# Two graph-attention layers on one core: new issue tables, no negated weights, other first loads and last operations

## The chip, the cores and the metric

The kernel runs on one core of one Trainium2 chip. The metric is the device time of one execution in microseconds (us), the smaller the better. All data are float32.

A core has five engines that run beside each other and wait for each other only through semaphores. TensorE (PE in the profile; its weight loads are PEld) multiplies matrices. VectorE (DVE), ScalarE (ACT) and GpSimd (POOL) do the elementwise work. SyncE (SP) issues DMA transfers; ACT and POOL can issue them too.

## The reference

There are 128 graphs of 128 nodes with 512 features each: `x` is (128, 128, 512) and `adj` is (128, 128, 128). Each layer is attention with 8 heads of 64 over the nodes of a graph, weighted by the adjacency:

```
layer 0:  q, k, v = x W_q + b_q, x W_k + b_k, x W_v + b_v
          e   = exp(q k' / 8 + c) * (adj + eps)      c, gate: from x and w_g
          x1  = x + gate * (e v) / rowsum(e)
layer 1:  q, k, v = x1 Wq + bq, x1 Wk + bk, x1 Wv + bv
          e   = exp(q k' / 8) * max(adj, 1e-8)
          o   = (e v) / rowsum(e)
          out = layernorm(x1 + o Wo + bo; gamma, beta)
```

That is seven projections of 16,384 rows by a 512 x 512 matrix, and 2 x 128 x 8 small attentions. A test on the row sums (`good`, `bad`) runs along and at the end decides on a branch that these inputs don't take.

## The kernel before, in words

**Tiles and stages.** Four graphs make a group (G = 4), 32 groups a layer (NG = 32). Group t runs from 0 to 63: 0 to 31 are layer 0, 32 to 63 layer 1. Per group the kernel loads x turned (features on partitions, tile `xT`) and natural (`xn`), forms sums of its blocks on POOL, makes v, q and k, scores, softmax weights and the mixed values. In layer 0 the result x1 goes to memory twice, natural (`x1d_n`) and in blocks of 32 x 32 (`x1d_b`). In layer 1 the mixed values go to memory in blocks and come back turned:

- `store_blocks` writes `x1d_o` in four stores of 128 KB (packets of 128 bytes) for each half of the group;
- `load_mixed` reads each half back into `GW` (512 KB, tile `gw`), and DVE transposes its 32 x 32 blocks;
- POOL forms sums (`innerB`, `innerT`), and `o_matrix` multiplies by Wo;
- `residual` adds x1 with an accumulating DMA of 512 KB on POOL's own queue (`h<-x1d_n`), two per group; `norm_and_store` normalises and stores.

All other transfers of the steady groups are issued by SP, in order, on one queue (q1).

**Strassen on two levels.** A projection is seven products of half-size blocks (class `Strassen`). P6 and P7 are multiplied plainly, P1 to P5 by seven quarter-size products each (`inner`). The weight side needs sums of weight blocks: `combine_outer` (on DVE for layer 0's v, q and k, on POOL for layer 1) and `combine_inner` (POOL). The x side needs `outer_sums` and `inner_sums` on POOL. In the kernel before, the weight block A22 was kept negated (`NA22`), by a `tensor_scalar_mul` in `combine`.

**Order.** The function records every operation in an object `Plan`, which finds what must precede what. `tabled` gives each operation a due time out of a table and issues them by due time, as soon as their predecessors are out; `issue` (L523) does it, so nearly all lines of the trace are L526. This fixes each engine's program order; the hardware then only waits for semaphores. There are five tables of due times in hundredths of a microsecond: FIRST (groups 0 to 2), the pattern for groups 3 to 29 (one table with a start and a period), CHANGE (groups 30 to 35), the pattern for groups 36 to 60, and LAST (61 to 63 and the closing part). 20,907 operations are placed so.

**Places that the change touches.** The beginning of `fast_path`: the first loads of x (`load_natural(0)`), of W_v, W_q and W_k (`weights`), of w_g into `GW`, and of the row b_v (`ROW`), whose sum with the first v products runs on DVE. The change of layers: at group 32 `weigh_rows(c)`, for c from 0 to 3, builds b_v Wo from quarters of Wo in `GW[:, 2]`. The closing part: group 62's four graphs still need their layer norm (`HU`) while group 63 (`HL`) is worked graph by graph. `begin_one` and `finish_one` do the norm of one graph with two DVE instructions; `ordinary` does it with a scaling on ACT (`scale`) and two POOL instructions (`rows`), after a `shift` on POOL. The last instructions are the norm of graph 3 of group 63, its store, and the test `bad`.

Of the kernel before, what the change touches and what calls it, by code (L numbers as in the profile page):

```python
# [42 lines left out]
class Strassen:  # L43


    A11, A12, S4, NA22, S1, S2, S3 = range(7)
    OPERANDS = {
        "P1": (A11, "B11"), "P2": (A12, "B21"), "P3": (S4, "B22"), "P4": (NA22, "T4"),
        "P5": (S1, "T1"), "P6": (S2, "T2"), "P7": (S3, "T3"),
    }  # L50
    SUMS = {"T1": ("B12", "B11"), "T2": ("B22", "T1"), "T3": ("B22", "B12"), "T4": ("T2", "B21")}
    RAW = {(0, 0): A11, (1, 0): A12, (1, 1): NA22, (0, 1): S3}
    INSIDE = ("P1", "P2", "P3", "P4", "P5")

    @staticmethod
    def load(engines, t, w):

        q = w.rearrange("(k c p) (m e) -> k m p c e", k=2, p=P, m=2)
        for n, ((k, m), i) in enumerate(Strassen.RAW.items()):
            engines[n % len(engines)].dma_start(t[:, i], q[k, m])  # L60

    @staticmethod
    def combine(v, a11, a12, a21, na22, s1, s2, s4, part=None):


        if part != 1:
            v.tensor_tensor(s1, a21, na22, ALU.add)
            v.tensor_tensor(s2, s1, a11, ALU.subtract)
        if part == 0:
            return  # L70
        v.tensor_tensor(a21, a11, a21, ALU.subtract)
        v.tensor_tensor(s4, a12, s2, ALU.subtract)
        v.tensor_scalar_mul(na22, na22, -1.0)

    @staticmethod
    def combine_outer(v, t, part=None):
        w = Strassen
        w.combine(v, *(t[:, i] for i in (w.A11, w.A12, w.S3, w.NA22, w.S1, w.S2, w.S4)), part)
# [10 lines left out]
    def inner_weight(t, x, i):  # L89
# [13 lines left out]
    (3, 29, 71.95, 41.905, [int(v) for v in '''  # L103
        0 2091 1819 2159 3282 230 115 1491 1245 2355 2023 2457 1887 2274 3842 1559 2389 1423 1955 3593 6418 4033
        4374 5817 9269 9422 5963 6533 3925 4295 5277 4424 3674 4548 5140 5208 5071 5401 5916 5847 5470 5682 5516
        5984 6537 7217 6661 7498 7301 8277 7582 7836 8361 8644 7933 9588 9748 10550 9913 10045 10788 5025 5081 5149
        5176 5213 5281 5344 5412 5475 5522 5650 5694 5738 5803 5888 5105 5257 5354 5381 5432 5500 5585 5653 5781
        5828 6059 6190 6234 6529 6680 5917 6146 6215 6241 6299 6385 6442 6525 6573 6619 6652 6738 6806 6833 6870
        6938 7001 7070 7111 7157 7228 6753 6914 7173 7200 7367 7452 7498 7763 7859 7906 6595 6783 6801 6820 7740
        6343 6886 6916 6960 7425 8271 8679 7872 8789 7982 7133 7653 8094 7369 7534 8582 8821 8840 8859 8947 7717  # L110
        8431 8518 8734 9071 9202 9312 9469 9694 9579 13385 11897 13425 6422 6485 6554 6580 6693 6761 6826 6895 7045
        7091 7137 7410 7454 7585 7629 7754 7800 6706 6782 6850 6877 6958 7026 7067 7289 7345 7391 7881 7947 7991
        8078 8340 8386 7470 7541 7610 7636 7673 7742 7816 7884 7925 7971 8025 8122 8190 8217 8254 8322 8385 8453
        8494 8541 8673 8432 8516 8600 8627 8680 8800 8987 9055 9097 9143 7978 8034 8103 8129 8209 8277 8341 8409
        8472 8519 8564 8724 8768 8855 8899 8967 9013 8058 8165 8234 8261 8297 8366 8429 8497 8560 8612 9118 9184
        9228 9315 9383 9471 8726 8811 8880 8907 8943 9012 9053 9121 9162 9209 9262 9359 9427 9454 9491 9624 9688
        9773 9819 9865 9936 9517 9578 9651 9678 9731 10140 10293 10361 10468 10514 10037 10449 10596 10274 10387
    '''.split()]),
    (36, 60, 1503.84, 52.968, [int(v) for v in '''
        0 1486 1548 492 2912 3531 445 3872 4580 5040 4709 3569 3679 4902 5164 5274 5526 5347 5868 4374 5233 5416  # L120
        5595 4153 4276 4295 4055 4184 4214 4587 4697 4367 4477 4405 4827 5030 4641 4771 5174 5297 5450 4988 5176
        5306 5632 5946 5522 5836 8015 11828 13160 4196 4361 4429 4456 4660 4729 5087 5155 5404 5450 5535 5645 5798
        5885 5953 4526 4704 4783 4810 4945 5185 5360 5428 5513 5560 6104 6169 6278 6322 6390 5632 5688 5756 5783
        5841 5910 5972 6041 6147 6194 5922 6016 6084 6111 6235 6303 6366 6434 6497 6543 6614 6450 6519 6587 6614
        6694 6762 6825 6906 6956 7003 5698 5754 5822 5849 5929 5997 6060 6128 6213 6294 6340 6453 6563 6650 6781
        6850 6895 6266 6410 6478 6505 6606 6675 6869 6937 7022 7068 6978 7087 7240 7284 7352 7398 6687 6738 6806
        6833 6912 6981 7044 7129 7175 7221 7309 7371 7472 7498 7546 7640 7699 7768 7852 7899 7981 7444 7503 7571
        7598 7656 7724 7809 7960 8094 8148 7075 7131 7199 7226 7328 7405 7459 7527 7590 7636 7682 7765 7874 7962
        8005 8086 8132 7141 7197 7265 7292 7415 7557 7612 7680 7743 7789 8203 8247 8400 8487 8555 8601 7862 7918
        7986 8013 8050 8118 8159 8270 8378 8424 8058 8116 8184 8215 8291 8359 8444 8512 8575 8649 8731 8647 8695  # L130
        8776 8803 9024 9092 9155 9280 9330 9420 8812 9177 9301 9048 9161 5079 5931 6324 6327 7282 7343 7569 7698
        6407 7890 7426 7500 8384 8140 8208 10130 10268 10754 7822 8577 9836 8935 8232 8334 8402 8429 8531 8599 8640
        8710 8782 8889 9067 9111 9199 9549 9653 8504 8597 8675 8702 8739 8807 9242 9490 9636 9750 10045 10088 10154
        10198 10266 9149 9286 9354 9521 9592 9713 9914 10047 10132 10187 10513 10570 10638 10665 10723 10807 10898
        10983 11029 11075 11146 10339 10427 10496 10540 10613 10682 10766 10835 10876 10922 11004 12447 13042 12723
        12845 13327 13341 13362 13574 13743 13915 14342 13595 13750 14039 14473 11862 13338 13436 12875 13400 13464
        13497 13588 13667 14015 14590 14719 14117 14843 15008 15401
# [3 lines left out]
        1538 7625 29872 1229 1777 0 0 47 47 141 141 188 94 94 914 470 517 0 410 484 510 584 460 534 560 645 423 235  # L141
        799 752 4549 705 611 1620 658 564 3469 1233 329 4220 4293 376 26047 21079 24140 7653 14131 706 886 1006 1619
        1870 1126 1438 2293 2051 2826 2706 3007 3420 3788 3668 851 980 727 1414 1104 1479 1249 1381 1653 2858 1885
        2280 3298 4667 2800 3277 5251 5481 4451 4604 5553 610 653 697 741 826 1178 1222 1265 1309 1377 872 916 1003
        1091 1558 1484 1528 1572 1615 1739 1047 1353 1397 1440 1810 1921 1965 2009 2052 2171 2271 2315 2490 2577
        2645 545 2106 2677 2152 2050 2009 2276 2759 2322 3075 2194 4245 4163 5113 2363 2420 2466 3132 2512 3242 1797
        2553 1844 4907 5760 785 828 959 1134 1443 1541 1746 1790 2096 2140 2244 2342 1659 1703 1834 1878 1990 2533
        2621 2665 2708 2776 2822 2358 2402 2446 2839 2946 3058 3102 3145 3233 3360 3189 3277 3495 3539 3607 1373
        2924 4369 5719 5195 4286 4948 5375 6230 4616 2635 5416 4328 6065 3422 5636 6783 6866 7031 7363 2235 2594
        4673 3034 5926 2883 2927 2971 3014 3082 3128 3364 3408 3451 3583 3651 3714 2184 2227 2752 2796 3176 3845  # L150
        3889 3932 3976 4044 4090 3626 3714 3801 4064 4138 4238 4282 4370 4413 4504 4195 4844 4931 4975 5136 3861
        5885 4989 6024 6520 1566 1612 5983 2718 7265 5030 6617 7584 7321 7893 4204 4575 6825 7419 6727 4122 5154
        5678 5595 8459 4632 4969 5217 4868 5017 961 1348 1029 846 2232 1484 1416 1165 1667 2413 1850 1097 2054 1918
        3237 1552 1735 1986 1280 3298 7196 8688 3218 7308 8755 9468 3516 282 3479 3608 4783 3737 2965 3173 4012 3902
        4714 5526 5458 5816 3971 4081 5071 4410 6271 6663 6395 6557 8266 8445 7460 7630 8922 9243 8142 8383 9386
        9518 8640 8774 9590 3687 3758 3826 3853 4020 4088 4151 4281 4326 4372 4457 4501 4544 4888 4956 3249 3320
        3389 3415 3670 3908 4107 4199 4348 4443 5106 5150 5194 5237 5336 4516 4588 4729 4756 5019 5196 5325 5397
        5511 5588 4576 5063 5131 5158 5675 5808 5850 5918 5959 6005 6087 5409 5467 5568 5594 5719 5787 5893 6066
        6193 6271 5369 5580 5664 5829 6106 5533 5656 5674 5693 7072 8619 7203 9353 7543 7309 5981 6456 6715 6327
# [369 lines left out]
def fast_path(ctx, tc, args, GOOD, bad):  # L529
# [3 lines left out]
    nc = Plan(tc)  # L533
# [816 lines left out]
```

## Time and profile before

| | |
|---|---|
| median of 3 runs | 3109.75 us (3105.86 to 3109.96) |
| profiled execution, own time | 3109.7 us |
| its span | 3107.9 us, granted clock 0.998 |
| PE busy | 3061.0 us, 98% |
| DVE, POOL, ACT busy | 2290.9, 2240.3, 1803.5 us |
| DMA | 341.87 MB, q1 42.1% and q0 (POOL's) 6.3% of 16 engines' span |
| longest groups | layer 0: a period of 41.9 us; layer 1: of 53.0 us |

The span is the time from the first to the last instruction of the profiled execution; 1.8 us of the own time lie around it. Busy times say how long an engine was at work, not whether it was waited for. As nearly all instructions stand on one line, the profile is read by tiles and by windows of time here, one window for each group or stage.

### The profile page before, as it was taken

How to read it: one execution, taken by the hardware profiler on the slowest of the kernel's cores; microseconds unless marked ns; L12 is line 12 of the kernel's file. 1: busy time of each engine (PE TensorE's matmuls, PEld its weight loads, DVE VectorE, ACT ScalarE, POOL GpSimd, SP SyncE). 2: the span in 40 equal slices, each digit the busy share in tenths (PEclk: the TensorE clock that was granted, in tenths of full speed). 3: DMA queues.
4: the chain of work that ended last, by engine and by line, in shares of the span. 5: the costliest groups of instructions: out<-in, count | busy, mean ns of one | idle time of the engine just before them, and what ended most of it. 6: DMA issues, size and time to landing. Idle time of an engine off the chain costs nothing.

```text
span 3107.9 us, 121261 instructions
## 1 busy us (share of the span) xinstructions
PE 3061.0 (98%) x50394; PEld 2665.0 (86%) x50394; DVE 2290.9 (74%) x5075; ACT 1803.5 (58%) x5179; POOL 2240.3 (72%) x2713
## 2 busy tenths in 40 slices
PE   8999999999999999999999999999999999999997
PEld 6888888888888888878888888888888888888885
DVE  5777777777777777766777777777777777777776
ACT  3666666666666666644555556565655555555653
POOL 8777666667666666689686867777786868687775
PEclk9999999999999999999999999999999999999999
DMA  4655555555555555444435353535444453535343
GB/s 117 129 118 112 112 116 117 113 124 113 111 108 118 114 120 117 100 134 103 105 95 123 86 131 81 124 87 123 94 113 105 102 115 93 124 83 130 81 106 101
DMA packets 963098, 341.87 MB, mean 110 GB/s; under 512 B 864240, under 2 KB 871408, under 8 KB 962544
## 3 DMA queue, kind: packets, MB, share of 16 engines
q1 hardware_dynamic: 944272, 299.48, 42.1%
q0 software_dynamic: 16864, 32.51, 6.3%
q8 instruction: 396, 6.49, 0.9%
q10 hardware_dynamic: 1408, 2.10, 0.2%
q14 instruction: 158, 1.29, 0.1%
HBM read 192.42 MB, written 141.56 MB: 107 GB/s over the span
## 4 chain that ended last, share of the span: by engine, by line
PE 74%; POOL 11%; DMA 8%; SPq 2%; issue 2%; DVE 2%; ACT 1%; ACTq 0%; POOLq 0%; DVEq 0%
PE bankA L526 36%; PE s L526 13%; PE bankB L526 13%; PE bankC L526 13%; DMA x1d_o<-o 4%; POOL h L526 3%; DMA gw<-x1d_o 3%; POOL T L526 2%; SPq L526 2%; POOL innerB L526 1%; POOL xn L526 1%; POOL innerT L526 1%; DVE gw L526 1%; ACT h L526 0%; POOL xT L526 0%
## 5 line engine op out<-in xcount | busy, mean ns | idle before, releaser
L526 PE MATMUL bankA<-T,w 128*64 128x256 f32 (+1 forms) x4232 | 541.0, 351 | 1.1 <-ACT bankA L526 1.1
L526 DVE TENSOR_TENSOR bankA<-bankA,s 128x128 f32<-128x128 f32 x868 | 255.5, 295 | 325.8 <-PE bankA L526 199.4
L526 PEld LDWEIGHTS bankA<-T,w 128*64 128x64 f32 x4232 | 273.2, 137 | 37.5 <-ACT bankA L526 1.6
L526 ACT ACTIVATE bankA<-ident 128x256 f32<-128x256 f32 x434 | 168.1, 387 | 197.4 <-DVE v L526 61.9
L526 POOL TENSOR_TENSOR gw<-xn,gw 128x512 f32<-128x512 f32 x128 | 162.9, 1279 | 162.0 <-ACT gw L526 93.5
L526 POOL TENSOR_TENSOR gw<-w,gw 128x512 f32<-128x512 f32 x128 | 163.5, 1283 | 155.3 <-ACT gw L526 110.2
L526 PE MATMUL bankA<-w,T 128*64 128x256 f32 (+1 forms) x2116 | 273.4, 351 | 0.0
L526 DVE TENSOR_TENSOR bankB<-bankB,s 128x128 f32<-128x128 f32 x650 | 191.2, 294 | 104.2 <-PE bankB L526 92.1
L526 PE MATMUL s<-qT,kT 64*128 64x128 f32 x4096 | 263.1, 278 | 0.0
L526 PEld LDWEIGHTS s<-qT,kT 64*128 64x128 f32 x4096 | 238.6, 188 | 28.3 <-issue 22.3
L526 DVE TENSOR_TENSOR bankC<-bankC,s 128x128 f32<-128x128 f32 x652 | 191.2, 293 | 96.4 <-PE bankC L526 48.8
L526 PE MATMUL bankC<-xT,w 128*64 128x128 f32 (+1 forms) x2296 | 229.2, 279 | 0.1
L526 ACT COPY s<-bankA 128x128 f32<-128x128 f32 x434 | 114.6, 264 | 192.4 <-PE bankA L526 135.8
L526 ACT ACTIVATE gw<-gw 128x512 f32<-128x512 f32 x256 | 161.6, 632 | 109.1 <-POOL gw L526 109.1
L526 ACT ACTIVATE bankC<-ident 128x256 f32<-128x256 f32 x326 | 125.0, 383 | 163.3 <-DVE v L526 50.2
L526 POOL TENSOR_TENSOR xn<-gw 128x512 f32<-128x512 f32 x62 | 79.3, 1279 | 137.2 <-PE bankA L526 131.9
L526 DVE STREAM_TRANSPOSE xT<-xT 128x512 f32<-128x512 f32 x252 | 173.3, 696 | 2.4 <-issue 2.4
L526 ACT ACTIVATE s<-s,c 128x1024 f32<-128x1024 f32 x128 | 139.7, 1092 | 55.2 <-PE s L526 55.2
L526 PE MATMUL bankA<-w,xn 128*64 128x256 f32 x1364 | 168.3, 350 | 0.0
L526 ACT COPY s<-bankB 128x128 f32<-128x128 f32 x325 | 86.4, 266 | 139.6 <-PE bankB L526 137.8
L526 PEld LDWEIGHTS bankC<-xT,w 128*64 128x64 f32 x2296 | 142.1, 137 | 25.3 <-ACT bankC L526 16.0
L526 POOL TENSOR_TENSOR innerB<-gw 128x256 f32<-128x256 f32 x31 | 22.5, 727 | 194.7 <-DVE gw L526 194.7
(268 smaller groups left out, 10183.8 us busy)
## 6 DMA issues: line engine op xcount, KB each, us to landing
xT<-x1d_b SPq DMA_DIRECT2D x64, 512.0 KB, 4.8
xT<-in_x_dram SPq DMA_DIRECT2D x496, 64.0 KB, 3.6
x1d_o<-o SPq DMA_DIRECT2D x248, 128.0 KB, 3.9
gw<-x1d_o SPq DMA_DIRECT2D x62, 512.0 KB, 4.3
h<-x1d_n POOLq DMA_DIRECT2D x62, 512.0 KB, 8.0
out_dram<-h SPq DMA_DIRECT2D x60, 512.0 KB, 3.9
xn<-in_x_dram SPq DMA_DIRECT2D x32, 512.0 KB, 4.7
x1d_b<-w SPq DMA_DIRECT2D x128, 128.0 KB, 3.5
```

The lines of the kernel that those rows point to most:

```text
L526: self.tc.keep_in_program_order(getattr(getattr(self.nc, engine), method)(*args, **kw))
```

## The change

It has five parts.

1. **No negated weights.** A22 is kept as loaded; the sum T4 is B21 − T2 in place of T2 − B21. The `tensor_scalar_mul` of `combine` is gone: 39 on POOL (35 of 128x128, 4 of 128x512) and 3 on DVE (128x512).
2. **First loads.** x and W_v are loaded by turns, two halves of x and two quarters of W_v at a time, on SP and ACT; the row b_v follows at once, ahead of W_q.
3. **`weigh_rows(0)`** runs on ACT in place of DVE (two instructions of 128x256).
4. **Last operations.** Graphs 3 and 0 of group 62 take `ordinary` after one more `shift`, in place of `begin_one` and `finish_one`: four DVE instructions become two on ACT and four on POOL (five with the shift), and the store of graph 3 goes from ACT's to SP's issue.
5. **New tables.** All five tables of due times are others. The matmuls are the same in number and shape, 25,181 calls; 20,868 operations are placed in all. The periods stay at 41.905 and 52.97. In layer 1's pattern, counted from the group's first `xT` load, the transfers and what follows them are due at:

| due after the first xT load, us | before | after |
|---|---|---|
| two `residual` loads, POOL's queue | 4.1, 12.7 | 1.05, 3.11 |
| last four `x1d_o` stores | 2.25, 3.35, 5.39, 6.49 | 2.39, 3.03, 3.67, 4.31 |
| second reload `gw<-x1d_o` | 10.30 | 8.75 |
| DVE's transposes of it | 19.85, 20.46 | 16.79, 17.40 |
| POOL's first sum from it | 21.29 | 18.23 |

The second xT load and the adjacency are due at 4.96 and 5.41 after the change.

```diff
     def combine(v, a11, a12, a21, a22, s1, s2, s4):
+        v.tensor_tensor(s1, a21, a22, ALU.add)
+        v.tensor_tensor(s2, s1, a11, ALU.subtract)
         v.tensor_tensor(a21, a11, a21, ALU.subtract)
         v.tensor_tensor(s4, a12, s2, ALU.subtract)
-        v.tensor_scalar_mul(na22, na22, -1.0)
...
-    SUMS = {"T1": ("B12", "B11"), "T2": ("B22", "T1"), "T3": ("B22", "B12"), "T4": ("T2", "B21")}
+    SUMS = {"T1": ("B12", "B11"), "T2": ("B22", "T1"), "T3": ("B22", "B12"), "T4": ("B21", "T2")}
...
-    (3, 29, 71.95, 41.905, [int(v) for v in '''
+    (3, 29, 75.15, 41.905, [int(v) for v in '''
...
-    (36, 60, 1503.84, 52.968, [int(v) for v in '''
+    (36, 60, 1510.52, 52.967, [int(v) for v in '''
...
-CHANGE = 18.03, [int(v) for v in '''
+CHANGE = 16.42, [int(v) for v in '''
...
-LAST = 2828.05, [int(v) for v in '''
+LAST = 2830.01, [int(v) for v in '''
...
-            nc.gpsimd.tensor_tensor(t4, t2, b21, ALU.subtract)
+            nc.gpsimd.tensor_tensor(t4, b21, t2, ALU.subtract)
...
             if c == 0:
-                nc.vector.tensor_scalar(o, w, b, None, ALU.mult)
+                nc.scalar.activation(o, w, AF.Identity, scale=b)
...
-    load_natural(0, nc.sync, nc.scalar)
-    weights(WV, 0, 0, w_v0, nc.sync, nc.scalar)
+    for k in range(2):
+        load_natural(0, nc.sync, nc.scalar, pairs=(k,))
+        weights(WV, 0, 0, w_v0, nc.sync, nc.scalar, quarters=slice(2 * k, 2 * k + 2))
+    nc.sync.dma_start(ROW, b_v0.partition_broadcast(P))
     weights(WQ, 0, 1, w_q0)
...
     load_adjacency(0)
-    nc.sync.dma_start(ROW, b_v0.partition_broadcast(P))
...
-    begin_one(u, 3, HU[3])
-    finish_one(u, 3, HU[3])
+    shift(u, slice(0, 2))
+    ordinary(3)
...
-    begin_one(u, 0, HU[0])
-    finish_one(u, 0, HU[0])
+    ordinary(0)
```

## The prediction

> **What bounds the kernel now.** I read first the page's busy times and its chain of work, then the windows query over single groups, then the waits, the timeline and the chain of waits wherever a window showed TensorE short of full.
>
> ```profile
> PE 3061.0 (98%) x50394; PEld 2665.0 (86%) x50394; DVE 2290.9 (74%) x5075; ACT 1803.5 (58%) x5179; POOL 2240.3 (72%) x2713
> PE 74%; POOL 11%; DMA 8%; SPq 2%; issue 2%; DVE 2%; ACT 1%; ACTq 0%; POOLq 0%; DVEq 0%
> ```
>
> TensorE is busy for 3061.0 of 3107.9 us. The change leaves every matmul in place, so it can win only TensorE's idle time: 46.9 us, of which about 15 lie behind the last real matmul. The chain says who holds it up: POOL and DMA, hardly DVE. Where it idles is read from windows of one group each (columns: window, length, then busy us of PE, PEld, DVE, ACT, POOL, granted clock, DMA share, GB/s):
>
> ```profile
> 0.00:71.95 71.95, 63.40 (x736) 47.74 (x738) 40.91 (x69) 21.95 (x58) 59.80 (x99) 1.00 0.54 127
> 71.95:113.86 41.91, 41.91 (x708) 36.97 (x704) 28.93 (x67) 27.34 (x77) 36.64 (x47) 1.00 0.60 126
> 1371.00:1413.00 42.00, 36.48 (x436) 26.62 (x434) 25.81 (x40) 9.12 (x21) 35.84 (x54) 0.96 0.09 14
> 1821.60:1874.60 53.00, 51.35 (x855) 45.11 (x850) 38.77 (x88) 29.04 (x82) 38.06 (x47) 1.00 0.47 107
> 2139.50:2192.40 52.90, 52.90 (x885) 46.87 (x883) 40.60 (x92) 30.92 (x88) 39.76 (x50) 1.00 0.46 107
> 3039.90:3092.90 53.00, 49.63 (x602) 35.15 (x600) 37.13 (x78) 21.54 (x59) 36.24 (x44) 1.00 0.32 82
> 3092.90:3107.90 15.00, 0.19 (x2) 0.09 (x2) 8.36 (x16) 0.98 (x5) 3.80 (x5) 0.64 0.39 143
> ```
>
> Layer 0's steady group is full (41.91 of 41.91), so a new pattern there can win nothing. In layer 1 some groups are full (2139.50) and some are not (1821.60). The rest of the loss is in the start, the change of layers and the end.
>
> The start, from TensorE's timeline (in brackets: idle before, and what ended it):
>
> ```profile
> 8.77 1.95 PE L526 MATMUL bankA<-w,xT 128*64 128x256 f32 x16 [1.65 <-DMA w<-in_L_gnn_W_v_dram]
> 16.03 1.95 PE L526 MATMUL bankA<-w,wi 128*64 128x256 f32 x16 [1.44 <-DVE w L526]
> 20.61 0.65 PE L526 MATMUL bankA<-w,wi 128*64 128x256 f32 x4 [1.34 <-DVE u L526]
> 50.53 0.44 PE L526 MATMUL bankC<-w,xT 128*64 128x128 f32 x4 [2.97 <-POOL xT L526]
> ```
>
> That is 7.4 us in four stalls. Behind the second and third is DVE's `t<-bankA,row`, which sat 3.57 us until the row b_v landed at 14.50; the row is only the 13th load on SP.
>
> The change of layers, all engines:
>
> ```profile
> 1370.05 0.46 POOL L526 TENSOR_TENSOR wi<-w,wi 128x128 f32<-128x128 f32 x1
> 1370.06 6.30 DVE L526 TENSOR_SCALAR gw<-w,bv 128x256 f32<-128x256 f32 x1
> 1372.51 3.71 POOL L526 TENSOR_TENSOR w<-w 128x512 f32<-128x512 f32 x3
> 1376.28 0.68 DVE L526 TENSOR_TENSOR v<-bankB,u 128x512 f32<-128x512 f32 x1
> 1377.06 0.69 PE L526 MATMUL bankB<-w,xT 128*64 128x256 f32 x2 [5.52 <-issue]
> ```
>
> `weigh_rows(0)`'s product takes 6.30 us while POOL runs sums without a break; its twin at 1381.78 takes 0.31. Behind it in DVE's order is the v sum that frees bank B, and TensorE idles 5.52 us.
>
> Layer 1, from the chain of waits:
>
> ```profile
> 1851.07 8.91 DMA x1d_o<-o
> 1860.04 7.11 DMA gw<-x1d_o
> 1867.81 0.67 DVE gw L526
> ```
>
> The mixed output goes to memory in blocks and comes back: store 8.91, reload 7.11 (the page's medians are 3.9 and 4.3), and then DVE's transpose starts late. Counted from the first xT load of each group, the second reload lands at 20 to 22 us in most groups and DVE is ready for it at about 20.3: no margin. The TensorE gaps that follow are 0.1 to 1.6 us and sum to about 7.5 over groups 36 to 60.
>
> The tail:
>
> ```profile
> 3091.86 1.75 DVE L526 SCALAR_TENSOR_TENSOR xT<-xT,rs,beta 128x512 f32<-128x512 f32 x1 [0.87 <-POOL rs L526]
> 3101.04 0.34 ACTq L526 DMA_DIRECT2D out_dram<-h  x1
> 3101.41 0.14 DVE L526 TENSOR_SCALAR bad<-bankC 1x1 int32<-1x1 f32 x1 [0.28 <-PE bankC L526]
> ```
>
> After the last real matmul (3092.6) DVE's normalisations run to 3101, then `bad`, and 6.35 us after `bad` the span ends; the last store lands at 3103.10, before that.
>
> **What the Trainium skill says.** "VectorE: DVE Perf Modes", section "Mode 2×_2P — use both read ports for one tensor": a product of one SBUF tensor with a scalar takes both of VectorE's read ports. "GPSIMD Engine Reference", section "1. Specifications": GpSimd shares its SBUF interfaces with VectorE, and contends with such an instruction or with one of two SBUF inputs. The trace agrees: 6.30 against 0.31 us. "DMA: Bandwidth & Descriptors", section "Queues, rings and completion order": each DMA engine takes turns between queues packet by packet. The trace fits: stores of 128-byte packets on q1, 3.9 us by median, take about 9 whenever `residual`'s 512 KB load on POOL's queue runs beside them.
>
> **The change part by part** (us against the profiled execution: span 3107.9, own time 3109.7, which is also the median of the three runs, 3109.75).
>
> *No negated weights.* POOL loses 35 products of 0.53 and 4 of 1.49, 24.5 us; DVE loses 3 of 0.66 to 0.96. T4 = B21 − T2 costs what T2 − B21 did. In the steady groups there are none of these, and the windows there are full: 0. Before the stall at 47.6 lie five of POOL's, 2.8 us; at the change of layers (1345 to 1413) lie seven, 7.1 us, counted with the parts below.
>
> *First loads.* W_v's first quarter takes the place of a load that landed at 7.02; the first product starts about 7.5 in place of 8.77 (−1.3), then waits some 0.6 for the next quarter (on ACT's queue, behind two x loads, at about the rate seen, 290 to 300 KB/us). The row comes 7th on SP in place of 13th, at about 11 us, before its use at 13: the stalls of 1.44 and 1.34 go (−2.8). But TensorE then reaches the sums of the next group 3.5 us earlier, and POOL, late for it by 2.97 already, is relieved of only 2.8 and of some DVE collisions: I keep 1.8 of that stall (−1.2). Sum **−4.7**; bounds −2 (POOL still sets the time at 47 us) and −8.
>
> *`weigh_rows(0)` on ACT.* Two activations of 128x256 at about 0.39 (row `bankA<-ident`, 387 ns) on an engine that is busy 9.12 of 42 us there. The DVE instruction and its collision go: **−5.5**. What waits instead: an ACT instruction now waits for a W_o quarter, and the bank copies queued behind it on ACT wait too. The new order issues the quarter 5.9 us ahead of its use, loads of that kind took 2.7 to 5.3, so I take 0; a late load would cost at most some 3. The nearby stalls are 1.13 at 1282 and 0.27 and 0.47 at 1354; only the last two have one of POOL's products (1.49) ahead of them, so I take these and nothing for the first: **−0.8** (0 to −1.9).
>
> *New order in layer 1.* The two `residual` loads go from 4.1 and 12.7 us after the group's first xT load to 1.05 and 3.11; the four stores from 2.25–6.49 to 2.39–4.31, and now stand ahead of the second xT load and the adjacency (4.96, 5.41); the second reload goes from 10.30 to 8.75, and DVE's transposes from 19.85 to 16.79 (due times of the two tables; the trace of before keeps to its own, counted so, within some 0.6 us). So the reload must land 3.1 us earlier. In group 36 of the trace both residual loads stand early (4.6, 6.4): all transfers are drained at 17.4 and the reload lands 3.3 later. With the loads 3.4 earlier that becomes 14.0 and, the reload's latency uncovered, 17.3: just in time. But there the stores were last of all; with 768 KB of large packets behind them they end near 12.5, the reload follows those 768 KB at about 14.1 and, at 1.5 us for 512 KB, lands near 16.2. Margin 0 to 1.1 us in place of 0: I take half of the stalls or a little more, **−4**; bounds −7.5 (all) and, the rival below, +20.
>
> *End.* The same reload gaps in the last groups (2.33 at 3041.4, 0.57, some small) should go with the earlier reload, with 2 us more between reload and use: **−3** (0 to −3.5). Four DVE instructions of 0.74 become two ACT scalings and five POOL operations, four of 1.28. DVE's chain shortens; POOL beside it slows it again (1.75 against 0.74 above). In the new order the test `bad` runs well ahead of the last store, so the end is that store, its 2.1 us of landing and about 1 more, in place of `bad` plus 6.35: **−1.8** (0 to −3).
>
> Sum: −4.7 −5.5 −0.8 −4 −3 −1.8 = −19.8, that is 3109.7 − 19.8 = 3089.9; I say **3090**.
>
> **The rivals.**
> 1. *The stores starve (slower).* Two residual loads now run beside all four stores, not two, and the packets take turns: if the stores land at 14 to 15 as in the trace, the reload lands near 18.5 and TensorE waits in every group. For it: group 36. Against it: the loads start earlier and less stands before the stores. Each late us costs 25 over groups 36 to 60: the other gains (15.8) plus today's 7.5 are eaten at 0.93 us a group; at 1.2 it is 3116. Chance 0.1.
> 2. *Only the DVE collision counts.* POOL keeps the start where it is, the reload stays without margin, the tail gives nothing: −5.5 −0.8 for the change of layers, −2 for the start, −1.5 for the end, which is 3099.9. For it: POOL ends the stall at 50.5 today. Chance 0.2.
> 3. *Everything comes.* All stalls named go: −8 −5.5 −1.9 −7.5 −3.5 −3 = −29.4, 3080. Chance 0.15.
> 4. *The change does nothing on balance*: the new order has stalls of its own, as long as today's. Against it: same products, and layer 0's full windows, leave it few places. Chance 0.06.
>
> The forecast has the remaining 0.49. A difference of 0.2% (6.2 us) is about what a measurement tells from none. Faster takes cases 2, 3, the forecast: 0.83; same takes case 4 and a part of 1: 0.08; slower 0.09. Range 3079 to 3102: case 3 below, case 2 with a few us of late reloads above.
>
> **What would show it.** Right: no gap above 1 us before 22 us; a gap of under 2 near 45 to 50; no DVE instruction of 6 us near 1370 and an ACT activation `gw<-w` of 0.4; windows of layer 1 at 52.9 to 53.0 TensorE, with `gw<-x1d_o` landing at or before 17.3 after the first xT load; TensorE's last real matmul near 3075; a tail under 14 us. Wrong: TensorE gaps behind DVE `gw` in each group of layer 1 (rival 1), ACT waiting for W_o, or a POOL stall near 47 us as long as before.

## The result, and the profile after

The changed kernel takes 3164.64 us (median of 4 runs, 3162.64 to 3165.73) against 3109.86 (4 runs): a ratio of 1.0178, 95% interval 1.016 to 1.0195. It is 55 us slower. I had forecast 20 us faster, with 3102 as the upper end and 0.09 for slower. Its profiled execution took 3164.67 us, with a span of 3162.8.

The page of the kernel after, busy times and chain of work:

```profile
PE 3074.8 (97%) x50394; PEld 2685.3 (85%) x50394; DVE 2289.2 (72%) x5066; ACT 1800.1 (57%) x5183; POOL 2219.9 (70%) x2679
PE 78%; DMA 8%; DVE 4%; SPq 4%; POOL 3%; issue 2%; ACT 1%; ACTq 0%; DVEq 0%; POOLq 0%
```

Two things differ from before. TensorE, with the same 50,394 instructions, is busy 13.8 us longer; and POOL's share of the chain has gone from 11% to 3%, while DMA and SP's queue have stayed or grown. So POOL was relieved, as the change meant, and the time went elsewhere. The windows, by stage, in the columns of the prediction (window, length, busy us of PE, PEld, DVE, ACT and POOL, granted clock, DMA share, GB/s):

```profile
0.00:71.95 71.95, 67.30 (x818) 51.62 (x820) 44.58 (x73) 27.31 (x72) 63.10 (x98) 1.00 0.55 126
1355.00:1397.00 42.00, 41.56 (x512) 29.65 (x510) 22.67 (x41) 11.66 (x26) 41.47 (x64) 1.00 0.06 19
1958.00:2011.00 53.00, 50.03 (x824) 44.69 (x818) 38.04 (x87) 28.05 (x82) 35.39 (x46) 0.97 0.39 97
2135.60:2188.60 53.00, 52.45 (x865) 46.12 (x861) 40.00 (x90) 30.26 (x87) 38.84 (x49) 1.00 0.45 106
3094.30:3147.30 53.00, 52.38 (x668) 39.33 (x664) 38.85 (x82) 25.26 (x68) 39.71 (x48) 1.00 0.33 90
3147.30:3162.80 15.50, 0.09 (x2) 0.00 (x0) 9.06 (x12) 1.77 (x7) 6.39 (x6) 0.61 0.38 139
```

In the start TensorE is busy for 67.30 us where it was for 63.40; at the change of layers it is busy nearly all the time, and in the last stretch too. Layer 1 is not: 50.03 of 53.00 in one group, at a granted clock of 0.97.

The same is seen by counting: when does TensorE reach its n-th instruction in both traces (the totals are the same)? The difference at the same count, stage by stage, beside the prediction's terms:

| stage (time in the kernel before) | forecast | measured |
|---|---|---|
| start, to 100 us | −4.7 | −4.5 |
| steady layer 0, to 1262 | 0 | −1.7 |
| change of layers, to 1453 | −6.3 | −7.1 |
| layer 1, to 3021 | −4 | +72.2 |
| end, to the last real matmul | −3 | −4.2 |
| tail | −1.8 | +0.2 |
| sum | −19.8 | +54.9 |

Now layer 1 in one group. The chain of waits of the kernel after (start, length, what):

```profile
1974.44 6.24 DMA x1d_o<-o
1980.76 4.66 DMA gw<-x1d_o
1986.08 0.67 DVE gw L520
```

SP's own timeline in that group:

```profile
1965.37 0.34 SPq L520 DMA_DIRECT2D xT<-x1d_b  x1
1967.87 8.38 SPq L520 DMA_DIRECT2D x1d_o<-o  x4
1976.29 2.62 SPq L520 DMA_DIRECT2D xT<-x1d_b  x1
1978.96 0.43 SPq L520 DMA_DIRECT2D adjT<-x1d_a  x1
1980.76 0.32 SPq L520 DMA_DIRECT2D gw<-x1d_o  x1
```

The four stores take SP 8.38 us to issue, not the 2 of the table. Nearly five of these go into the third alone, whose issue ends 0.9 us after the first store has landed; that the queue was full until then is inferred, not shown. What stands behind them on SP is late too: the second xT load goes out 10.9 us after the first, not 5. The reload is issued as soon as the last store has landed, at 15.4; it lands at 20.1, and DVE waits. TensorE's timeline shows the price:

```profile
1987.00 0.69 PE L520 MATMUL bankA<-xT,wi 128*64 128x128 f32 x4 [2.97 <-DVE bankA L520]
```

There is a gap in every group, from 0.5 to 4.6 us; the gaps between 1455 and 2965 sum to 62.1 us (10.0 before). And a long gap is paid for again. Two gaps of the kernel after, of 2.97 and of 2.33 us, by windows (the clock is the third number from the right):

```profile
1984.00:1987.00 3.00, 0.03 (x3) 0.00 (x1) 1.55 (x4) 0.48 (x3) 0.17 (x1) 0.99 0.06 25
1987.00:1988.00 1.00, 1.00 (x10) 1.00 (x12) 0.80 (x3) 0.00 (x0) 0.85 (x2) 0.50 0.00 0
1990.00:1991.00 1.00, 1.00 (x20) 1.00 (x18) 0.40 (x2) 0.70 (x3) 0.39 (x1) 0.83 0.00 0
1991.00:1992.00 1.00, 1.00 (x22) 0.93 (x18) 0.73 (x4) 0.99 (x2) 0.99 (x3) 1.00 0.00 0
1928.40:1930.80 2.40, 0.08 (x2) 0.00 (x0) 1.54 (x4) 0.53 (x3) 0.15 (x1) 1.00 0.01 3
1930.80:1932.00 1.20, 1.19 (x22) 1.19 (x24) 1.10 (x5) 0.07 (x1) 1.04 (x3) 1.00 0.00 0
```

After the long gap TensorE runs at half clock for 3.4 us, with half as many matmuls in a microsecond (10 for 20 to 22), and so loses 1.7; after the short one it loses nothing. Eleven gaps of the kernel after are followed by that, one of them (4.64 us, at 1591) for 6.8 us. An estimate from these figures, twelve times 1.7, is 20 us; before had one such stretch in its groups' work, behind the 5.52 us gap. That is more than the 13.8 us by which the busy time grew.

### The profile page after: what moved, and what is told of

Read it like the earlier page. It is cut to its first block, busy times and chain, and to the rows that moved or that the text cites. A ratio compares the mean times of both kernels' runs of the same rounds, so it can differ in the third digit from the quotient of the medians.

```text
span 3162.8 us, 121314 instructions
## 1 busy us (share of the span) xinstructions
PE 3074.8 (97%) x50394; PEld 2685.3 (85%) x50394; DVE 2289.2 (72%) x5066; ACT 1800.1 (57%) x5183; POOL 2219.9 (70%) x2679
## 3 DMA queue, kind: packets, MB, share of 16 engines
q0 software_dynamic: 16864, 32.51, 6.2%
## 4 chain that ended last, share of the span: by engine, by line
PE 78%; DMA 8%; DVE 4%; SPq 4%; POOL 3%; issue 2%; ACT 1%; ACTq 0%; DVEq 0%; POOLq 0%
PE bankA L520 37%; PE s L520 14%; PE bankB L520 14%; PE bankC L520 13%; SPq L520 4%; DMA x1d_o<-o 4%; DMA gw<-x1d_o 3%; DVE h L520 1%; POOL T L520 1%; POOL w L520 1%; POOL wi L520 1%; DVE xT L520 1%; DVE gw L520 1%; ACT h L520 0%; DVE o L520 0%
## 5 line engine op out<-in xcount | busy, mean ns | idle before, releaser
L520 PE MATMUL bankA<-w,T 128*64 128x256 f32 (+1 forms) x2116 | 265.0, 352 | 0.0
L520 PEld LDWEIGHTS s<-qT,kT 64*128 64x128 f32 x4096 | 238.6, 188 | 29.3 <-issue 20.1
L520 ACT ACTIVATE bankB<-ident 128x256 f32<-128x256 f32 x325 | 125.5, 386 | 82.8 <-DVE u L520 27.9
L520 ACT ACTIVATE s<-s 128x1024 f32<-128x1024 f32 x128 | 124.0, 1006 | 77.3 <-PE s L520 77.3
L520 PEld LDWEIGHTS bankC<-xT,w 128*64 128x64 f32 x2296 | 143.6, 138 | 24.9 <-ACT bankC L520 16.9
```

The costliest lines, as they stand in the source:

```text
L520: self.tc.keep_in_program_order(getattr(getattr(self.nc, engine), method)(*args, **kw))
```

## The experiments

Theory S: the residual loads, which now both stand beside the stores, make the stores, SP's queue and so the reload late. Rival R: the new order simply asks for the reload too early. In what follows, times of transfers are medians over groups 36 to 59, counted from the group's first xT load, and runs of "before" are those on the same chip. Labels name the kernels.

**h_later**: the second residual load later in the order. The edit is one number in the row of the layer-1 table that holds `norm_and_store`'s operations (and the same for group 35).

```diff
-        12663 12644 12759 12780 13283 13600 12880 13159 13407 13731 10904 13021 13782 13239 13432 13866 14241 14128
+        12663 12644 12759 12780 13283 13600 12880 13159 13407 13731 11884 13021 13782 13239 13432 13866 14241 14128
```

> After, with one entry of the layer-1 pattern changed: the second residual load of each group (h<-x1d_n) due 12.9 us after the first xT load in place of 3.1 (and the same entry of group 35). Theory S (the second residual load takes turns with the stores x1d_o<-o and holds SP's queue back): the reload gw<-x1d_o lands at 17 or before, TensorE's stalls behind DVE's gw go from 61 us to under 10, the clock dips behind them go, and the time is 3095 (3088 to 3104). Rival R (the transposes stand 3.1 us too early in the new order, whatever the residual loads do): the reload lands at 18 or later, stalls of 1 us or more in each group stay, 3130 or more.

Measured: 3107.92 (before 3107.23; ratio 1.0005, 0.9995 to 1.0016). The 55 us are back, from one moved load, but not the 13 more that S promised. The stores end at 11.2 in place of 14.8, yet the reload lands at 17.7. POOL's timeline tells why:

```profile
2062.15 0.46 POOL L520 TENSOR_TENSOR inner<-gw 128x128 f32<-128x128 f32 x1
2062.55 1.24 POOL L520 DMA_DIRECT2D h<-x1d_n  x1
2071.07 0.72 POOL L520 TENSOR_TENSOR innerB<-gw 128x256 f32<-128x256 f32 x1 [7.28 <-DVE gw L520]
```

A due time fixes only the order on the engine. POOL was idle, so it issued the load 10.7 us after the first xT load, not 12.9, and the load ran beside the reload, which then took 6.4 us where it takes 4.2 in the kernel after.

**before_h_early**: the same load, earlier in the old order.

```diff
-        12845 13327 13341 13362 13574 13743 13915 14342 13595 13750 14039 14473 11862 13338 13436 12875 13400 13464
+        12845 13327 13341 13362 13574 13743 13915 14342 13595 13750 14039 14473 11162 13338 13436 12875 13400 13464
```

> Before, with one entry of the layer-1 pattern changed: the second residual load due 5.7 us after the first xT load in place of 12.7. Theory S: the last two stores land near 16 in place of 14, the reload near 21 to 22 in place of 20 to 21, stalls of 0.7 to 1.5 us more in each of 25 groups: 3127 to 3147. Rival R: the old order's later transposes leave room for it, 3104 to 3116.

Measured: 3111.7 (before 3107.23; ratio 1.001, 1.0001 to 1.0018), in R's range. The last store is later by 2.5 us (17.1 against 14.6), as S said, but the reload only by 0.4 (20.8 against 20.45), for without a load beside it, it takes 3.6 in place of 5.8. So S alone is not enough: what such a load takes from the stores it gives back to the reload. It hurts where the reload is wanted early.

**plain_copy, plain_second, plain_first**: what is it about these loads? These kernels move the same bytes but leave out the addition, so their outputs lack the residual. The edit is for plain_copy; the other two make it for the second or for the first load only.

```diff
-        nc.gpsimd.dma_start(HSB[k], X1D[split(t)[1]][2 * k : 2 * k + 2].rearrange("b p d -> p b d"), accum_op=ALU.add)
+        nc.gpsimd.dma_start(HSB[k], X1D[split(t)[1]][2 * k : 2 * k + 2].rearrange("b p d -> p b d"))
```

> After, with the residual loads as plain copies without accumulation (the residual is left out). If the accumulation is what makes these loads heavy, they finish in half the time, stalls are under 0.5 us a group, and the time is near 3100. If it is the taking of turns between two queues, whatever the operation, stalls of over 1 us a group stay and the time is above 3140.

> After, with only the second residual load of each group as a plain copy (half of the residual is left out). If the second load alone, beside the stores, makes the loss, the time is within 10 us of plain_copy's 3077.5; if both do, or only the first, it lies half way to after's 3164.6 or above, over 3110.

> After, with only the first residual load of each group as a plain copy (half of the residual is left out); the second accumulates. With both plain the time was 3077.5, with the second plain 3093. If the second is the one that hurts, 3125 to 3155; if the two hurt only together, under 3100.

Measured, one run each: 3077.45, 3092.96 and 3101.91. The queue table of the page, of after and then of plain_copy:

```profile
q0 software_dynamic: 16864, 32.51, 6.2%
```

```profile
q0 software_dynamic: 8928, 32.51, 3.6%
```

The same bytes in half the packets and little over half the DMA time: the accumulation is what makes the loads heavy. Waits of DVE on the reload (us, times, longest), of after and of plain_copy:

```profile
DVE gw L520 <- DMA gw<-x1d_o: 66.6, 28, 4.8
```

```profile
DVE gw L520 <- DMA gw<-x1d_o: 0.5, 1, 0.5
```

The time of plain_copy is also below the 3100 that I expected. The times don't add up: either load made plain brings back 63 to 72 us of the 87 that both bring. (Neither plain_second nor plain_first came out at an end that I had written down: the one is 15 us from plain_copy, not under 10 and not over 3110; the other is between the 3100 and the 3125 of its two ends.) The landings come close to adding up:

| | reload lands | DVE's transposes start | time |
|---|---|---|---|
| none accumulates (plain_copy) | 15.84 | 16.76 | 3077.5 |
| first only (plain_second) | 17.16 | 17.18 | 3093.0 |
| second only (plain_first) | 17.51 | 17.53 | 3101.9 |
| both (after) | 19.08 | 19.10 | 3164.7 |

The first accumulation delays the reload by 1.3 to 1.6 us, the second by 1.7 to 1.9. DVE comes to the transposes at 16.8. What lands before that costs nothing; what lands after costs its lateness, and a long gap costs the clock as well. R and S are each half of the cause: that DVE asks at 16.8 is R's half, that the reload lands at 19.1 is S's.

**before_act**: one part of the change alone, in the old order.

```diff
-                nc.vector.tensor_scalar(o, w, b, None, ALU.mult)
+                nc.scalar.activation(o, w, AF.Identity, scale=b)
```

> Before, with weigh_rows(0) on ACT in place of DVE and nothing else. By the prediction the 5.52 us gap at 1371 goes, and TensorE is 5 to 6 us ahead of before from 1413 on, to the end: 3104.3. Rival: the time comes back as another wait (ACT on the W_o quarter, or POOL) and TensorE is less than 2 us ahead at 1500.

Measured: TensorE is 5.9 us ahead behind 1453 of where it was at 1345 (instruction for instruction). The 5.52 us gap is gone; two later lines of its timeline:

```profile
1371.64 0.90 ACT L526 ACTIVATE gw<-w,bv 128x256 f32<-128x256 f32 x2
1405.23 0.44 PE L526 MATMUL bankA<-w,xT 128*64 128x128 f32 x4 [0.93 <-POOL xT L526]
```

0.93 comes back behind POOL, and the half clock behind the old gap is saved as well. In the whole time (3107.23, one run; before 3107.23, from 3101.8 to 3116.34 over 31 runs) it can't be seen. In this one trace 3.4 us of it are lost again by 3021, in layer 1, which the edit doesn't touch; why is not shown.

**h_after_reload and dve_back**: the load behind POOL's first sum from the reload, with the statistics moved along (the first edit); then that with the DVE product put back (the second edit too).

```diff
-        12663 12644 12759 12780 13283 13600 12880 13159 13407 13731 10904 13021 13782 13239 13432 13866 14241 14128
+        12663 12644 12759 12780 13283 13600 12880 13159 13407 13731 12429 13321 13782 13379 13432 13866 14241 14128
...
-                nc.scalar.activation(o, w, AF.Identity, scale=b)
+                nc.vector.tensor_scalar(o, w, b, None, ALU.mult)
```

> After, with the second residual load of layer 1's groups 36 to 60 placed behind POOL's first sum from the reload (due 18.36 after the first xT load in place of 3.1) and the statistics that need it 3.0 and 1.4 us later; group 35 as in h_later. In h_later POOL was idle and issued that load at 10.8, not 12.9, beside the reload, which then took 5 to 8 us. Theory S: now nothing accumulates beside stores or reload, the reload lands by 17, stalls behind DVE's gw are under 5 us in all, and the time is 3082 (3076 to 3090). Rival P: POOL, busy without a break from 19 us on, is late by the 1.24 us of the issue, and TensorE waits for POOL in each group: 3098 to 3112.

> h_after_reload with weigh_rows(0) back on DVE and nothing else. If the collision of DVE's product with POOL's sums is the cause, TensorE stands 3 to 6 us longer near 1360 to 1375 than in h_after_reload; if it was the old order that made it long, less than 1 us.

Measured: h_after_reload 3120.67 (before 3106.55; ratio 1.0044, 1.0027 to 1.0061). The reload lands at 15.8 and DVE no longer waits for it, as S says; but every group has a gap of 0.97 us of another kind. POOL's timeline, then ACT's, then TensorE's:

```profile
1645.79 1.24 POOL L520 DMA_DIRECT2D h<-x1d_n  x1
```

```profile
1650.05 0.81 ACT L520 ACTIVATE h<-h,rs 128x512 f32<-128x512 f32 x1 [1.90 <-POOL rs L520]
1650.77 0.37 ACT L520 ACTIVATE bankC<-ident 128x256 f32<-128x256 f32 x1
```

```profile
1651.18 0.44 PE L520 MATMUL bankC<-inner,wi 128*64 128x128 f32 x4 [0.97 <-ACT bankC L520]
```

Issuing the load costs POOL 1.24 us; POOL's short rs operations come that much later, ACT waits for them with a scaling that nobody is in a hurry for, and behind it in ACT's order stands the operation that readies bank C for TensorE. Rival P named this rightly, though the time is 9 us above its range. In dve_back (3118.89, one run) the DVE products took this:

```profile
L520 DVE TENSOR_SCALAR gw<-w,bv x2: 348/636/924, 1348.3 to 1360.0; 128x256 f32<-128x256 f32 x2
```

At most 0.92 us, and TensorE stood no longer than in h_after_reload: at the instruction that before reaches at 1400 it is 16.9 us ahead of before, there 16.1. So in the new order the edit brings nothing. Why the product is short there stays open, for POOL's sums run beside it here too. POOL is busy for 19.6 of the 20 us from 1344 to 1364; beside the products at 1348.28 and 1359.99 its timeline has:

```profile
1347.78 1.27 POOL L520 TENSOR_TENSOR w<-w 128x512 f32<-128x512 f32 x1
1349.00 1.32 POOL L520 TENSOR_TENSOR T<-xT,T 128x512 f32<-128x512 f32 x1
1359.63 1.02 POOL L520 TENSOR_TENSOR wi<-w 128x128 f32<-128x128 f32 x2
```

So POOL's sums beside such a product are not enough to make it take 6.30 us.

**h_after_shift**: the load a little further on.

```diff
-        12663 12644 12759 12780 13283 13600 12880 13159 13407 13731 10904 13021 13782 13239 13432 13866 14241 14128
+        12663 12644 12759 12780 13283 13600 12880 13159 13407 13731 12764 13561 13782 13659 13792 13866 14241 14128
```

> h_after_reload with the second residual load moved on behind POOL's two short rs operations (due 21.7 after the first xT load), so that ACT's scaling of the first half no longer waits for POOL, and the statistics that need it at 29.7 and 30.7. Theory S with P (in h_after_reload the reload was in time and the 0.97 us a group came from ACT queued behind POOL's rs): no stall behind gw, no stall behind ACT bankC, 3085 (3078 to 3096), faster than before. Rival: POOL's 1.24 us come out at its next user, some 0.5 to 1 us a group: 3098 to 3115.

Measured: 3115.11 (before 3107.93; ratio 1.0022, 1.0013 to 1.003), at the upper end of the rival's range. The gap behind ACT's bank C went, others came (most of them 0.47 us behind ACT's bank B), and the period of a group is 54.08 us in place of plain_copy's 52.83. That is 1.25 us more, and the issue holds POOL for 1.24. From 19 us after the first xT load to the end of the group POOL is busy for over 99% of the time, so there it has nothing to give.

**h_waits and h_waits_all**: the issue has to fall in POOL's idle time and yet after the reload. A small operation that reads the reload's tile makes POOL wait for it.

```diff
-    def load_blocks(to, src):
+    def load_blocks(to, src, tap=None):
         nc.sync.dma_start(to.rearrange("p b c n -> p (b c n)"), src.rearrange("q i b c t f -> (q i) (b c t f)"))
+        if tap is not None:
+            nc.gpsimd.tensor_tensor(tap, to[:, 0, 0, 0:1], to[:, 0, 0, 1:2], ALU.mult)
...
-            load_blocks(AT[t][:, 2 * k : 2 * k + 2], OB[t % 2][k])
+            load_blocks(AT[t][:, 2 * k : 2 * k + 2], OB[t % 2][k], TAP if k == 0 and NG + 3 <= t <= LAST - 5 else None)
...
-        12663 12644 12759 12780 13283 13600 12880 13159 13407 13731 10904 13021 13782 13239 13432 13866 14241 14128
+        12663 12644 12759 12780 13283 13600 12880 13159 13407 13731 11833 13021 13782 13239 13432 13866 14241 14128
```

> After, with the second residual load of groups 35 to 60 issued in POOL's idle time, but not before the reload has landed: a small new POOL operation (two numbers of gw, result unused) waits for the reload, and the load's issue stands right behind it (due 12.4 after the first xT load); group 35 as in h_later. Theory S with P (the loads must not run beside stores or reload, and POOL has no 1.24 us to give while it is busy): the reload lands near 15.5, the load is issued at 16 and lands at 22, before its statistics at 24.3; no stalls of over 0.3 us in groups 37 to 60, 3083 (3077 to 3092), faster than before by 0.5% or more. Rival: the wait in POOL's order, or the load beside what follows, costs a stall of its own: 3095 or more.

> h_waits, with the same treatment for groups 34 and 35, which keep their statistics 4 to 6 us later so that DVE doesn't wait for the load. In h_waits TensorE still lost 4.1 us at 1588 (DVE waits for group 35's load, which lands at 22.8 with its statistics due at 18.4) and about 1.7 in the clock behind it. Expected: that stall and the one at 1532 go, 3082 (3078 to 3088). If the stall only moves to the next user of that load, 3086 or more.

Measured: 3088.35 (before 3109.06; ratio 0.9933, 0.992 to 0.9947) and 3085.67 (before 3107.39; ratio 0.9926, 0.9913 to 0.994). Both beat both kernels. POOL's timeline of h_waits:

```profile
2013.70 0.19 POOL L520 TENSOR_TENSOR tap<-gw 128x1 f32<-128x1 f32 x1 [5.65 <-DMA gw<-x1d_o]
2013.92 1.25 POOL L520 DMA_DIRECT2D h<-x1d_n  x1
2015.41 0.73 POOL L520 TENSOR_TENSOR innerB<-gw 128x256 f32<-128x256 f32 x1 [0.24 <-DVE gw L520]
```

The reload lands at 15.7, the load is issued right behind it and done before POOL's sum could start anyway. The period is 52.85 in both, and between 1600 and 2850 neither has a gap over 0.3 us. In h_waits_all the stall at 1588 is gone; of that at 1532 a gap of 0.91 is left.

**end_back**: h_waits_all with the old last operations.

```diff
-    shift(u, slice(0, 2))
-    ordinary(3)
+    begin_one(u, 3, HU[3])
+    finish_one(u, 3, HU[3])
...
-    ordinary(0)
+    begin_one(u, 0, HU[0])
+    finish_one(u, 0, HU[0])
```

> h_waits_all with the last operations as before the change: graphs 3 and 0 of group 62 by begin_one and finish_one on DVE, without the shift, at the due times of the ACT and POOL operations that they replace. If those operations shorten the tail, as I forecast (1.8 us), the time from TensorE's last product of bank B to the end grows by 1 to 3 us from the 15.4 of h_waits; if POOL beside DVE takes back what DVE saves, it stays within 0.7 us.

Measured: 3081.27 (one run). From the end of TensorE's last bank B product to the end of the span it is 13.5 us, against 15.5 in h_waits_all, 15.5 in after and 15.3 in before. It is neither of what I wrote: in the new order the new operations lengthen the tail by 2 us, read from one trace each. (The whole time doesn't show it: one of the five runs of h_waits_all took 3081.5 too.) The tail of after, then that of end_back:

```profile
3147.47 2.81 DVE L520 SCALAR_TENSOR_TENSOR xT<-xT,rs,beta 128x512 f32<-128x512 f32 x2
3150.87 0.14 DVE L520 TENSOR_SCALAR bad<-bankC 1x1 int32<-1x1 f32 x1
3156.51 0.34 ACTq L520 DMA_DIRECT2D out_dram<-xT  x1
```

```profile
3067.05 1.40 DVE L520 SCALAR_TENSOR_TENSOR xT<-xT,rs,beta 128x512 f32<-128x512 f32 x2
3073.97 0.34 ACTq L520 DMA_DIRECT2D out_dram<-xT  x1
```

With POOL's long sums beside it, DVE's same two instructions take 2.81 in place of 1.40.

## Why the prediction was wrong

**The step that failed** is the sum for layer 1: "Margin 0 to 1.1 us in place of 0". I let the stores end near 12.5 and the reload land near 16.2. They end at 14.8 and it lands at 19.1 (medians). In it, three terms were wrong:

- The two residual loads were priced as 512 KB each, like any other load. Accumulating, they delay the reload by 3.2 us more than plain; plain_copy's 15.8 is close to my 16.2. The page of before held the hint, in the last column the median us to landing:

```profile
xT<-x1d_b SPq DMA_DIRECT2D x64, 512.0 KB, 4.8
h<-x1d_n POOLq DMA_DIRECT2D x62, 512.0 KB, 8.0
```

- I moved the transfers by their due times. The order put the second xT load and the adjacency at 5, SP came to them at 10 to 13, because it was still issuing the stores ahead of them. So "768 KB of large packets" did not run while the stores trickled; they ran late and ahead of the reload.
- I priced a late reload at its lateness. Eleven gaps were followed by half clock. TensorE's busy time in after is 23.9 us over that of plain_copy, some 20 of it by the estimate above from the clock, and 61.7 us are gaps. Together that is 85.6 of the 87.2 between the two. So it was also wrong that the change can win or lose only TensorE's idle 46.9 us: with the same 50,394 instructions its busy time is 3061.0 in before, 3074.8 in after and 3050.9 in plain_copy.

**The rival** "the stores starve" named the mechanism, its place and its point of decision rightly. I gave it 0.1 on the ground that less stands ahead of the stores and the loads start earlier. before_h_early shows what is true in that: in the old order, where DVE's transposes are due at 19.9, the same move costs under 5 us. The new order's earlier due time took the room away, and I had counted those 3.1 us only against my own landing estimate. The rival's price was too small as well: about 2.3 us of gap a group, plus the clock.

**Right**: the start (−4.5 for −4.7), with the stalls that I named left over. TensorE's timeline of after:

```profile
9.21 1.52 PE L520 MATMUL bankC<-w,xT 128*64 128x256 f32 x12 [0.81 <-DMA w<-in_L_gnn_W_v_dram]
21.47 1.95 PE L520 MATMUL bankA<-wi,w 128*64 128x256 f32 x16 [0.75 <-ACT t L520]
47.03 0.44 PE L520 MATMUL bankA<-w,xT 128*64 128x128 f32 x4 [1.62 <-POOL xT L520]
```

I had written 0.6 for the first and 1.8 for the last; only the 0.75 was not foreseen. No run takes the first loads, the missing negations or the start's new table alone, so how the three share the 4.5 is not shown. The change of layers (−7.1 for −6.3) was right in size, but its reason is only half shown: alone in the old order the move to ACT brings 5.9, in the new order it brings nothing, and a product beside POOL's sums took 0.92 there, not 6.30. The end (−4.2 for −3) is right in size; no run tests its reason. With layer 1 mended, the kernel is at 3085.67, near the forecast of 3090: of the six terms one was wrong by far, and it decided.

**Wrong as well, but small**: the tail. That `bad` would run well ahead of the last store came true: in after it starts 12 us before the end. But I put the end about 3 us behind that store's issue, and it is 6.3: 4.0 to landing in place of 2.1, and 2.3 more. The operations moved to POOL also cost DVE more than they save it. Layer 0's steady groups gave 1.7 us where I had taken none.

## What to carry to other kernels

An order is only as good as its model of transfers: before moving a load beside others, price it by its own row in the trace (an accumulating load is not a load of its bytes), and ask when its queue comes to it, not when it is due. A deadline with no slack turns into a stall one for one, so look for the time at which the consumer is ready and compare it with every landing that the move shifts. Where an issue must come late but its engine is idle, give the engine something to wait for; in h_later a later place in the order alone left the issue at 10.7 us in place of 12.9.

## What was not expected of the hardware

- The length of a gap alone doesn't tell whether TensorE's clock falls. In the kernel after it fell to 0.50 behind a gap of 2.36 us and not behind one of 2.54. In before, the start's gap of 2.97 us behind POOL was followed by full clock; in before_h_early, whose start is the same, a gap of 2.97 at the same place was followed by half clock. The 3.41 us behind it, in before and then in before_h_early (matmuls in brackets, clock third from the right):

```profile
50.53:53.94 3.41, 3.41 (x42) 2.67 (x44) 1.97 (x5) 0.00 (x0) 3.41 (x9) 1.00 0.20 77
50.04:53.45 3.41, 3.41 (x26) 2.31 (x24) 1.08 (x4) 0.00 (x0) 3.41 (x9) 0.50 0.20 77
```

  In all 14 traces the clock changes only at steps of 3.41 us, whose phase differs from run to run. Within these steps, at full clock, TensorE idled for 2.24 us or more in 24, and each was followed by a step at 0.50; it idled for 1.2 to 1.97 us in 47, and one (1.82) was. By these counts it matters how much of a gap falls into one step: of the gap in before at most 1.58 us did, of that in before_h_early 2.68. A step at half clock costs about 1.7 us.
- An accumulating load of 512 KB on POOL's queue has twice the packets of a plain one (16,864 against 8,928 on that queue in the whole run) and took 9.85 us to landing beside the stores, where the plain one took 5.9.
- Issuing such a load holds POOL for 1.24 us, where a plain one holds it for 0.7 to 0.8; the page counts this in POOL's busy time. Where POOL has no idle time, the period of a group grew by as much (54.08 against 52.83).
